# Two attention blocks: where the second sums of four weights are made, and which tiles hold them

## Chip, cores and metric

The kernel runs on one core of one Trainium2 chip. The metric is the device time of one execution, in microseconds (us). The kernel before was timed three times; one more execution was taken with the hardware profiler.

## The reference

The input x has 8 images of 512 channels and 32 x 32 = 1024 tokens. Two attention blocks follow each other:

```
layer 0: h = group_norm(x, 32 groups); q, k, v = w_qkv h + b      (8 heads of 64 channels)
         x = x + w_proj softmax(q k / 8) v + b_proj
layer 1: h = group_norm(x, 8 groups);  q, k, v = w h + b          (1 head of 512 channels)
         x = x + p_w softmax(q k / sqrt(512)) v + p_b
```

All of it is in 32-bit floating point.

## The kernel before

The matrix products with weights are not done directly. Each weight and each activation is split into 2 x 2 blocks, and seven products of sums of blocks replace eight products of blocks. `prepare(n)` loads a weight into a tile of the pool `wpool` and returns four steps, sums of its blocks on DVE (lines 285 and 286). For images after the first, the convolutions split once more: each of the seven operands is again cut into 2 x 2, with four further sums, the *second sums*. `keep2(n, t)` makes these for the weights v, q, k and m (four instructions of 128x896 on POOL, line 306) and stores the seven parts to DRAM, from which later images load them (line 308, seven DMAs called `sums_v`, `sums_q`, `sums_k`, `sums_m` in the profile; the profile calls the second sums by the name of the weight tile that they read, `prepare_v` and so on).

There are two pools that matter here. `big` has 32 tiles of 4 KB per partition and holds images, queries, keys, values, exponentials and factors. `wpool` has three tiles of 14 KB per partition and holds weights.

`prologue()` does the work before the first attention, in this order: load the layer 1 weights k and q and image 0, prepare v, q and k, multiply q and k to m (`product`, ps_wm), normalise image 0, make its block sums (`image_factors`, lines 170 to 173), then

- the value convolution of image 0 (`by_token`, bank names psa_v, psb_v, psc_v), whose steps p = 1, 2, 5, 6, 7, 4, 3 each run four pieces of a background list on DVE: the eight block sums of the image, then the first sums of q, then those of k,
- `keep2("v")`, the loads of image 1 for its statistics (x1, `bn_stats` at line 98),
- the q convolution (psa_q and so on), `keep2("q")` and `keep2("k")`,
- `prepare("m")` and the k convolution, with m's first sums between its steps, then `keep2("m")`,
- the load raw_p0, the transposes of layer 1's v weight (`natural`, tr_wv), their copies out of PSUM (natv, line 786, two on ACT and two on DVE), the mean of image 1 (gmean, d, d2, dv, lines 115 to 121), product z (ps_wz), products with biases.

In a convolution the sums u and w (line 238) go through DVE: the step p = 7 needs u, the step p = 4 needs w, since they share the PSUM bank b. After the prologue a loop over the images does attention of layer 0, projection, layer 1 of the image before, and the convolutions of the next one.

`tc.keep_in_program_order` pins an instruction behind what was traced before it on its engine. All other instructions are put into an order per engine when the program is built, and each engine then runs its own order, waiting where data or a tile isn't ready. A tile of a pool is used again when all users of its last contents are done.

Of the kernel before, what the change touches and what calls it, by code (L numbers as in the profile page):

```python
# [9 lines left out]
F32 = mybir.dt.float32  # L10
# [5 lines left out]
P = 128  # L16
# [13 lines left out]
def two_attention_blocks_kernel(  # L30
# [8 lines left out]
    nc = tc.nc  # L39
# [136 lines left out]
    def main_path(ctx):  # L176
        big = ctx.enter_context(tc.tile_pool(name="big", bufs=NBIG))
        wpool = ctx.enter_context(tc.tile_pool(name="wpool", bufs=3))
# [6 lines left out]
        def big_tile(name, shape=(P, T)):  # L185
            return big.tile(list(shape), F32, tag="big", name=name)
# [4 lines left out]
        def acc_tile(name):  # L191
            return ps_acc.tile([P, HT], F32, tag="acc", name=name)
# [14 lines left out]
        def load_x(b, c, what):  # L207
            t = big_tile(f"{what}_{b}_{c}")
            nc.sync.dma_start(t, x[b, c * P : (c + 1) * P, :])
            return t  # L210
# [12 lines left out]
        def finish():  # L223
            while tail:
                tail.pop(0)()
# [48 lines left out]
        def weight_factors(t):  # L274
            return {p: t[:, ORDER.index(p), :, :] for p in range(1, 8)}

        def prepare(n):
            t = wpool.tile([P, 7, 2, C // 2], F32, tag="w", name=f"prepare_{n}")
            half = lambda kh, mh: weights[n][ts(kh, C // 2), ts(mh, C // 2)].rearrange("(k p) m -> p k m", p=P)
            f = weight_factors(t)  # L280
            for p, kh, mh in ((1, 0, 0), (7, 0, 1), (4, 1, 1), (2, 1, 0)):
                nc.sync.dma_start(f[p], half(kh, mh))
            _, steps = left_sums(
                [(f[1], f[7])], [(f[2], f[4])], (lambda j: f[5], lambda j: f[6], lambda j: f[3]),
                lambda *a: tc.keep_in_program_order(nc.vector.tensor_add(*a)),
                lambda *a: tc.keep_in_program_order(nc.vector.tensor_sub(*a)),
            )
            return t, steps
# [4 lines left out]

        wdram2 = {n: dram.tile([P, 7, 7, P], F32, name=f"sums2_{n}") for n in "qkmv"}

        def keep2(n, t):

            u = [big_tile(f"prepare2_{n}_{i}", (P, 7, P)) for i in range(4)]
            quarter = lambda k, i: t[:, :, k, ts(i, P)]
            a11, a21, a12, a22 = quarter(0, 0), quarter(0, 1), quarter(1, 0), quarter(1, 1)  # L300
            s1, s2, s3, s4 = u
            for dst, x, y, op in (
                (s1, a21, a22, ALU.add), (s2, s1, a11, ALU.subtract), (s3, a11, a21, ALU.subtract),
                (s4, a12, s2, ALU.subtract),
            ):
                tc.keep_in_program_order(nc.gpsimd.tensor_tensor(dst, x, y, op))
            for j, f in enumerate((a11, a12, s4, a22, s1, s2, s3)):
                nc.sync.dma_start(wdram2[n][:, :, j, :], f)

# [31 lines left out]
        def image_factors(h, uid, sub=nc.vector.tensor_sub):  # L341

            tiles = [pair_tile(f"t{i}_{uid}") for i in (1, 2, 4)]
            halves = lambda t: (t[:, :HT], t[:, HT:])
            return right_sums(
                [halves(t) for t in h[:2]], [halves(t) for t in h[2:]],
                [lambda j, t=t: t[:, j, :] for t in tiles], sub,
            )
# [415 lines left out]
        def raw(n, i):  # L764
            ts_ = [pair_tile(f"raw{n}_{h}") for h in range(2)]
            for kc in range(KC):
                nc.sync.dma_start(ts_[kc // 2][:, kc % 2, :], w[i, ts(kc, P), :])
            return [ts_[kc // 2][:, kc % 2, :] for kc in range(KC)]
# [10 lines left out]
        def natural(wt, nm, banks):  # L779
            ts_ = [pair_tile(f"nat{nm}_{h}") for h in range(2)]  # L780
            t = [ts_[o // 2][:, o % 2, :] for o in range(KC)]
            pt = [ps_tile(banks[o // 2], f"tr_w{nm}_{o}") for o in range(KC)]
            for kc in range(KC):
                for o in range(KC):
                    transpose(pt[o][:, ts(kc, P)], wt[kc][:, ts(o, P)], ident)
            spread(lambda o, copy: tc.keep_in_program_order(copy(t[o], pt[o])), KC)
            return t

        def product(lhs, rhs, nm, hooks=()):

            hooks = dict(hooks)
            ts_ = [pair_tile(f"prod{nm}_{h}") for h in range(2)]
            for ic in range(KC):
                ps = ps_tile("a", f"ps_w{nm}_{ic}")
                for kc in range(KC):
                    matmul(ps, lhs[kc][:, ts(ic, P)], rhs[kc], start=(kc == 0), stop=(kc == KC - 1))
                    if ic * KC + kc in hooks:
                        hooks[ic * KC + kc]()
                nc.scalar.copy(ts_[ic // 2][:, ic % 2, :], ps)
                if ic % 2:  # L800
                    nc.sync.dma_start(
                        products[nm][ts(ic // 2, C // 2), :].rearrange("(kc p) o -> p kc o", p=P), ts_[ic // 2]
                    )
# [18 lines left out]
        def prologue():  # L822
            raw_k = raw("k", 5)
            raw_q = raw("q", 4)
            h0 = [load_x(0, c, "h0") for c in range(KC)]
            first = {n: prepare(n) for n in "vqk"}
            wk = natural(raw_k, "k", ("a", "b"))
            wq = natural(raw_q, "q", ("c", "acc"))
            norm = GroupNorm(0, "0_0", pinned=True)
            for c in range(KC):  # L830
                norm.stats(c, h0[c])
            hf, steps = image_factors(h0, "h0_0")

            def normed():
                norm.affine(acc_tile("gvar_0_0")[:, :KC])
                for c in range(KC):
                    norm.apply(nc.scalar if c % 2 else nc.gpsimd, h0[c], h0[c], c)

            product(
                wq, wk, "m", {6: lambda: norm.group_mean(acc_tile("gmean_0_0")[:, :KC]), 9: normed},  # L840
            )
            raw_v = raw("v", 6)
            raw_p = raw("p", 7)
            for f in first["v"][1]:
                f()
            background.extend(steps)
            for n in "qk":
                background.extend(first[n][1])
            v = by_token(weight_factors(first["v"][0]), hf, "v0_0", middle=(2, 5, 6, 7), back=4)
            finish()  # L850
            run_background(len(background))
            keep2("v", first["v"][0])
            x1 = [load_x(1, c, "x1") for c in range(KC)] if B > 1 else []
            norm1 = GroupNorm(0, "0_1")
            background.extend(lambda c=c: norm1.stats(c, x1[c]) for c in range(len(x1)))
            q = conv(weight_factors(first["q"][0]), hf, pcols("bq0"), "q0_0")
            keep2("q", first["q"][0])
            keep2("k", first["k"][0])
            t, steps = prepare("m")
            k = conv(weight_factors(first["k"][0]), hf, pcols("bk0"), "k0_0", hooks=[[], [], [], [], steps])  # L860
            finish()
            keep2("m", t)
            raw_p0 = raw("p0", 3)
            wv = natural(raw_v, "v", "bc")
            norm1.group_mean(acc_tile("gmean_0_1")[:, :KC])
            product(wv, raw_p, "z")
            norm1.affine(acc_tile("gvar_0_1")[:, :KC])
            bias = bias_products([(wk, "bq1"), (raw_p, "bv1"), (raw_p0, "bv0")])
            later = []
            for n in "pz":  # L870
                t, steps = prepare(n)
                later.append(steps)
                later.append([lambda n=n, t=t: keep(n, t), load_weight])
            later.append([
                lambda: tc.keep_in_program_order(nc.vector.tensor_copy(ubias, bias[0])),
                lambda: tc.keep_in_program_order(nc.vector.tensor_add(obias[1], bias[1], pcols("bp1"))),
                lambda: tc.keep_in_program_order(nc.vector.tensor_add(obias[0], bias[2], pcols("bp0"))),
                load_weight,
            ])
            return lambda s, head: v[s // 2][:, s % 2, ts(head, 64)], q, k, norm1, later  # L880

        psum_pools("first", 2)
        v, q, k, norm0, later = prologue()
# [141 lines left out]
        for b in range(B):  # L1025
# [18 lines left out]
            if b > 0:  # L1044
                hf, t = image_factors(h, f"h1_{b - 1}", here)
                for i, fs in enumerate((t[:1], t[1:2], (t[2], t[4]), (t[6], t[3]), (t[5], t[7]), steps[:2], steps[2:4])):
                    extra[2 * i + 3] += fs
            elif B > 1:
                hf, t = image_factors(h, "h0_1", here)
# [15 lines left out]
            if b > 0:  # L1065
                gf, gsteps = layer1_scores(b - 1, inner)
                _, _, mean, affine = norm_hooks(norm1, f"1_{b}")
# [7 lines left out]
                if b + 1 < B:  # L1075
                    v, norm0 = values(b + 1, made["inner"])
                    q, k = keys_and_queries(b + 1, made["inner"], norm0, ())
            elif B > 1:
                v, norm0 = values(1, inner)
# [217 lines left out]
```

## Time and profile before

| | us |
|---|---|
| median of 3 runs (lowest, highest) | 2845.38 (2845.05, 2845.61) |
| profiled execution, its own time | 2846.31 |
| its span | 2844.5 |
| PE busy | 2817.1 |
| DVE busy | 2129.8 |
| POOL busy | 1259.7 |
| ACT busy | 943.1 |
| first matmul of the value convolution of image 0 | 25.96 |
| first matmul of the q convolution | 59.03 |
| first matmul of product z | 114.33 |
| first matmul of the first attention's scores | 134.56 |

Times inside the span count from its start. The profiled execution's time is 1.8 us more than its span. PE is TensorE, DVE VectorE, ACT ScalarE, POOL GpSimd, SP SyncE, which issues nearly all DMAs here. A row in order of time gives start, duration, engine, line, operation and shapes; several equal instructions in a row are merged (x3). Rows by stretches give the length, then for PE, weight loads, DVE, ACT and POOL the busy us with the number of instructions, then the granted TensorE clock as a share, the busy share of the DMA engines, and GB/s.

### The profile page before, as it was taken

What the parts mean: (1) busy time and instruction counts of PE and PEld (TensorE: products, weight loads), DVE (VectorE), ACT (ScalarE), POOL (GpSimd) and SP (SyncE); (2) the same over time, 40 slices, a digit from 0 to 9 for tenths busy, and PEclk for the clock granted to TensorE, in tenths of its full rate; (3) what the DMA queues carried; (4) which work ended last, traced back from release to release, by engine and by line L of the source; (5) the groups of instructions that cost most, each with busy time, mean ns of one, the idle gap of its engine ahead of it and who ended that gap; (6) DMA issues with size and microseconds to landing.
All of it is one profiled execution on the core that took longest, in us unless ns stands there. A gap on an engine that the chain in (4) does not pass through costs nothing.

```text
span 2844.5 us, 33986 instructions
## 1 busy us (share of the span) xinstructions
PE 2817.1 (99%) x12434; PEld 1694.7 (60%) x12434; DVE 2129.8 (75%) x2873; ACT 943.1 (33%) x1205; POOL 1259.7 (44%) x1253
## 2 busy tenths in 40 slices
PE   8999999999999999999999999999999999999998
PEld 5434834867358663676536775376843768338584
DVE  6388688776887768777787777877678776887765
ACT  1153363313532145221452215522154212633130
POOL 4114224852258422574216741277313772147672
PEclk9999999999999999999999999999999999999999
DMA  8543402144030430313303232122411224112301
GB/s 285 166 153 110 185 20 95 47 156 163 18 123 21 173 148 20 138 49 149 128 24 130 100 117 110 48 105 112 146 72 49 101 108 155 42 45 101 119 4 68
DMA packets 98851, 291.68 MB, mean 103 GB/s; under 512 B 10803, under 2 KB 42867, under 8 KB 88950
## 3 DMA queue, kind: packets, MB, share of 16 engines
q1 hardware_dynamic: 96886, 287.16, 28.0%
q10 hardware_dynamic: 1792, 2.29, 0.2%
q8 instruction: 100, 1.64, 0.2%
q14 instruction: 73, 0.60, 0.1%
HBM read 236.94 MB, written 52.47 MB: 102 GB/s over the span
## 4 chain that ended last, share of the span: by engine, by line
PE 96%; DVE 2%; issue 1%; DMA 0%; ACT 0%; POOL 0%; SPq 0%; DVEq 0%; POOLq 0%; ACTq 0%
PE sc L67 16%; PE av L67 16%; PE psb_av L67 6%; PE psb L67 5%; PE psa_av L67 4%; PE psc_av L67 4%; PE psc L67 3%; PE psa L67 3%; PE psb_z L67 3%; PE psb_p L67 3%; PE psb_k L67 3%; PE psb_g L67 3%; PE psb_v L67 3%; PE psb_q L67 2%; PE psa_p L67 2%; PE psa_z L67 2%
## 5 line engine op out<-in xcount | busy, mean ns | idle before, releaser
L635 DVE TENSOR_TENSOR sum<-sum,e 128x1024 f32<-128x1024 f32 x384 | 518.7, 1351 | 41.4 <-DVE sum L635 1.4
L631 ACT ACTIVATE e<-sc 128x1024 f32<-128x1024 f32 x512 | 476.0, 1051 | 79.2 <-PE sc L67 79.2
L67 PE MATMUL sc<-q,k 64*128 64x512 f32 x2048 | 456.8, 596 | 0.0
L67 PE MATMUL av<-e,v 128*64 128x512 f32 x2048 | 453.6, 595 | 0.0
L67 PEld LDWEIGHTS sc<-q,k 64*128 64x128 f32 x2048 | 191.6, 186 | 238.5 <-ACT e L631 109.1
L67 PEld LDWEIGHTS av<-e,v 128*64 128x64 f32 x2048 | 141.4, 137 | 304.3 <-issue 304.3
L597 POOL TENSOR_TENSOR all_recs<-all_recs,rc 128x256 f32<-128x256 f32 x72 | 63.9, 888 | 543.5 <-DVE rc L595 543.5
L654 POOL TENSOR_TENSOR a<-a,r 128x512 f32<-128x512 f32 x56 | 113.7, 2031 | 260.8 <-DMA r<-rows 245.5
L595 DVE RECIPROCAL rc<-sums 128x256 f32<-128x256 f32 x72 | 126.5, 1757 | 46.1 <-PE sums L67 24.7
L649 ACT COPY a<-av 128x512 f32<-128x512 f32 x64 | 37.5, 586 | 321.7 <-PE av L67 321.7
L633 DVE TENSOR_TENSOR sum<-e,e 128x1024 f32<-128x1024 f32 x64 | 78.8, 1232 | 57.1 <-ACT e L631 57.0
L67 PE MATMUL psb<-inner,inner_h 128*128 128x256 f32 x448 | 116.1, 382 | 0.8
L67 PE MATMUL psa_av<-e,z 128*128 128x512 f32 x256 | 113.3, 595 | 0.0
L412 POOL TENSOR_TENSOR inner_h<-h,inner_h 128x256 f32<-128x256 f32 x120 | 109.1, 909 | 3.4
L140 ACT ACTIVATE h<-h,b,s 128x1024 f32<-128x1024 f32 x62 | 78.5, 1270 | 87.9 <-DMA h<-in_x 70.5
L67 PEld LDWEIGHTS psb<-inner,inner_h 128*128 128x128 f32 x448 | 83.9, 190 | 16.6 <-POOL inner L427 3.5
L412 POOL TENSOR_TENSOR inner_h<-h 128x256 f32<-128x256 f32 x60 | 56.7, 944 | 77.3 <-ACT h L140 77.3
L460 ACT COPY psb_v<-psa_v 128x512 f32<-128x512 f32 (+1 forms) x28 | 14.5, 517 | 223.9 <-DVE o L755 141.6
L695 POOL TENSOR_TENSOR sum<-sum,e 128x1024 f32<-128x1024 f32 x32 | 76.2, 2380 | 27.2 <-ACT e L691 26.0
L67 PE MATMUL psb_g<-inner_h,w_m 128*128 128x256 f32 x336 | 85.9, 383 | 0.3
L533 POOL TENSOR_TENSOR v<-v,v 128x256 f32<-128x256 f32 x28 | 20.1, 727 | 142.7 <-DVE u_v L528 142.7
L412 POOL TENSOR_TENSOR inner_h<-t_h 128x256 f32<-128x256 f32 x90 | 79.1, 885 | 9.0 <-DVE t_h L170 9.0
(364 smaller groups left out, 5736.6 us busy)
## 6 DMA issues: line engine op xcount, KB each, us to landing
x<-in_x SPq DMA_DIRECT2D x36, 512.0 KB
h<-in_x SPq DMA_DIRECT2D x32, 512.0 KB
spill<-x SPq DMA_DIRECT2D x32, 512.0 KB
h<-spill SPq DMA_DIRECT2D x32, 512.0 KB
x<-spill SPq DMA_DIRECT2D x32, 512.0 KB
out<-x SPq DMA_DIRECT2D x64, 256.0 KB
w_p<-sums_p SPq DMA_DIRECT2D x8, 1792.0 KB
r<-rows SPq DMA_DIRECT2D x112, 128.0 KB
```

Source lines behind the costliest of these rows:

```text
L67: tc.keep_in_program_order(nc.tensor.matmul(*args, **kw))
L140: tc.keep_in_program_order(nc.scalar.activation(dst, src, AF.Identity, bias=b, scale=s))
L412: pin(nc.gpsimd.tensor_tensor(dst, x, y, ALU.subtract))
L533: nc.gpsimd.tensor_tensor(d, x, y, ALU.add)
L595: nc.vector.reciprocal(rc, sums)
L597: nc.gpsimd.tensor_tensor(all_recs, all_recs, rc, ALU.add)
L631: nc.scalar.activation(e, sc, AF.Exp, scale=(C // 8) ** -0.5)
L633: nc.vector.tensor_add(total, es[0], e)
L635: nc.vector.tensor_add(total, total, e)
L649: nc.scalar.copy(dst, av)
L654: nc.gpsimd.tensor_tensor(dst, dst, r, ALU.mult)
L695: on = lambda dst, x, y: lambda: tc.keep_in_program_order(nc.gpsimd.tensor_tensor(dst, x, y, ALU.add))
```

## The change

`keep2` gets an engine as an argument. With the default, POOL, its four sums go into one tile of `wpool` instead of four of `big`; so it is for q, k and m. For v it is called with VectorE: there the sums stay in four `big` tiles and are made by DVE, pinned at the place of the call, which is behind the last outputs of image 0's value convolution.

```diff
-        def keep2(n, t):
-
-            u = [big_tile(f"prepare2_{n}_{i}", (P, 7, P)) for i in range(4)]
+        def keep2(n, t, engine=nc.gpsimd):
+
+            if engine is nc.gpsimd:
+                u = wpool.tile([P, 4, 7, P], F32, tag="w", name=f"prepare2_{n}")
+                u = [u[:, i, :, :] for i in range(4)]
+            else:
+                u = [big_tile(f"prepare2_{n}_{i}", (P, 7, P)) for i in range(4)]
...
-                tc.keep_in_program_order(nc.gpsimd.tensor_tensor(dst, x, y, op))
+                tc.keep_in_program_order(engine.tensor_tensor(dst, x, y, op))
...
-            keep2("v", first["v"][0])
+            keep2("v", first["v"][0], nc.vector)
```

## The prediction

> **What bounds the kernel now.** I read the shares of the page first, then the chain of waits in order of time, then DVE, POOL and SP in order of time round the two places where the chain leaves PE early on, and last the busy time by stretches of 10 us. The page's chain, by engine:
>
> ```profile
> PE 96%; DVE 2%; issue 1%; DMA 0%; ACT 0%; POOL 0%; SPq 0%; DVEq 0%; POOLq 0%; ACTq 0%
> ```
>
> So only a PE gap that goes away shortens the span, and a new cost counts only where it opens one. From the first scores (134.6 us) to 269 us the chain is PE alone; the diff acts before that. There the chain has two holes (start, us, what):
>
> ```profile
> 45.44 3.15 DVE prepare_k L286 x2
> 48.60 0.61 DVE w_v L238
> ...
> 49.25 6.48 PE psb_v L67 x16
> ...
> 110.64 3.68 issue
> 114.33 16.65 PE ps_wz L67 x32
> ```
>
> Hole A: the value convolution waits for DVE, which still makes the k weights' first sums ahead of w_v. Hole B: product z waits for the copies of the transposed v weights (natv). DVE and POOL at these places (start, us, line, operation, shapes):
>
> ```profile
> 43.07 5.53 DVE L286 TENSOR_TENSOR prepare_k<-prepare_k 128x512 f32<-128x512 f32 x3
> ...
> 110.09 1.30 DVE L117 TENSOR_TENSOR d<-mv,gmean 128x4 f32<-128x4 f32 x1
> 111.43 2.00 DVE L119 TENSOR_TENSOR d<-d 128x4 f32<-128x4 f32 x1
> ...
> 113.54 1.28 DVE L786 COPY natv<-tr_wv 128x512 f32<-128x512 f32 x2
> ```
>
> ```profile
> 44.94 2.51 POOL L306 TENSOR_TENSOR prepare_q<-prepare_q 128x896 f32<-128x896 f32 x1
> ...
> 111.34 2.07 POOL L306 TENSOR_TENSOR prepare_m<-prepare_m,prepare_m 128x896 f32<-128x896 f32 x1
> ```
>
> The same 128x512 sum takes 0.68 us at 37.6 us, where POOL is idle, and 1.7 to 2.6 us at 26.4 to 36.4 and 41.3 to 48.6 us, where POOL makes the second sums of v and q (25.93 to 35.9 and 40.41 to 47.5 us). A 128x4 operation of 0.16 us takes 1.30 and 2.00 us at 110 us and ends when a POOL sum ends. POOL runs second sums of v from 25.93 us, far before their place in the program, since nothing stands ahead of them there. Each hole then costs more than its idle time:
>
> ```profile
> 50.00:60.00 10.00, 10.00 (x35) 8.00 (x34) 3.76 (x6) 0.00 (x0) 4.58 (x3) 0.76 0.94 267
> ...
> 110.00:120.00 10.00, 5.67 (x7) 2.46 (x8) 4.72 (x6) 0.63 (x2) 3.41 (x2) 0.66 0.60 183
> ```
>
> The granted clock (third from the end) falls to 0.76 and 0.66. Sixteen psb_v matmuls take 6.48 us instead of the 3.45 us of the next sixteen, and the 32 of product z 16.65 us instead of 32 x 0.429 = 13.73 (eight such take 3.43 us).
>
> **What the skill says.** SBUF — State Buffer, "Who interferes with whom": a DVE instruction with two SBUF inputs and a GpSimd one that reads SBUF exclude each other, and the later one blocks until the other ends; one with at most one SBUF input does not. The trace agrees on both: the rows above, and v<-psb_v,t_v (one input in PSUM) keeps 0.69 us at 55.77 beside a POOL sum at 55.34. TensorE: Matmul & The Clock Gate, "What's actually happening": after an idle window of about 3.4 us the clock halves until PE has been busy as long. The gaps of 4.69 and 4.47 us with their slow matmuls agree; the gap of 0.83 us at 40.0 shows none. VectorE: DVE Perf Modes, the errata section, gives (N+151)/0.96 ns for an fp32 tensor_tensor; the trace has 0.69 us at 512 and 1.225 us at 1024, as the formula does.
>
> **The change, part by part.**
>
> (1) POOL loses the four v sums (9.97 us at 25.93 to 35.9). The q sums now need a weight tile. The pool has three, held by v, q and k weights; the first to come free is v's, after the value convolution and the stores of its sums. So POOL stands idle from 25.9 to about 56 us, and the eight image sums, four q sums and four k sums on DVE run at 0.68 us. From 26.42: L171, L172, L173 end at 30.5, q at 33.2. PE's order is kept: psb_v p=6 runs 36.4 to 39.9; u_v is ready at 38.9 and 40.6; k sums 40.6 to 43.3; w_v at 44.0. PE p=7 ends at 43.3, waits 0.7 us, p=4 ends at 47.5 and p=3 at 50.9, without a slow clock. Before, q's first matmul started at 59.03. Gain 8.1 us: gaps of 0.83 and 4.69 shrink to 0.7, the clock gives 2.9 to 3.0, the rest is rounding of ends.
>
> (2) DVE gains four 128x896 sums behind v's last outputs: estimate (896+151)/0.96 = 1.09 us each, 4.4 us, 51.6 to 56.0. Bounds: 1.07 (1.225 us scaled by 896/1024) to 2.5 (what a DVE sum took at most beside POOL's, which has no work then); the work itself can't bring a gain. Behind them wait the statistics of x1 and u_q. PE needs u_q only for psb_q p=7, 13.7 us after q starts, at 64.6: slack 8, cost 0. Without that cover it would be 4.4.
>
> (3) The seven v stores keep their number; three need no sums. The other four are issued on SP from about 53 to 58 us (5.48 us for four before), and x1's four loads (3.94 us) behind them to 62, 2 us later than before while PE is 8 earlier. If the x1 statistics stay ahead of u_q in DVE's order, the first x1 (6.7 us from issue to use before) and its 1.5 us of statistics put u_q at about 66: a stall of 0 to 2 us. I take 0, since u_q's input is ready first.
>
> (4) q's sums on POOL: 56 to 64.3 (4 x 2.08), stores to about 70; k's take that tile again, 70.5 to 78.8, stores issued by about 81. The m loads take the tile of q (q convolution ends at 86.5 - 8.1 = 78.5) or that of k's sums (82). Four issues (4.26 us) and landing: 85 to 90 us. DVE wants them at 101.88 - 8.1 = 93.8: slack 4 to 9, cost 0. DVE beside POOL's q and k sums does one-SBUF-input work, so it isn't slowed. The m sums then find a free tile by 82; p's loads take k's tile at 99 and are used at 130.
>
> (5) Twelve of the large tiles fewer are asked for after v. SP in order of time:
>
> ```profile
> 86.69 1.92 SPq L282 DMA_DIRECT2D prepare_p<-in_w  x4
> 105.05 12.22 SPq L308 DMA_DIRECT2D sums_m<-prepare_m  x7
> 117.32 3.75 SPq L767 DMA_DIRECT2D rawp<-in_w  x4
> ```
>
> The last row is raw_p0, read straight from an input, yet it stands behind sums_m although SP was idle for 16 us before these. And natv's DVE copies, traced ahead of the mean's operations, stand behind them in DVE's order. I read both as tiles being given in program order: raw_p0's and natv's come after the four large tiles of the m sums. With m, q and k sums out of that pool they follow k's tiles directly, so natv's copies can stand ahead of the mean's four operations. They read PSUM and so don't mind POOL. Product z then starts about 0.7 us after the transposes (product m: 0.46 after) instead of 4.5: 3.8 to 4.0 us, plus 2.9 of clock: 6.8. Bounds of this part: 0 (order stays) and 7.2. POOL's m sums stay beside d and d2, which are needed only when product z ends.
>
> Sum: 8.1 + 6.8 = 14.9 us off the profiled execution's 2846.31 (span 2844.5 and 1.8 around it), which is 0.9 above the median: median 2845.4 - 14.9 = 2830.5. Later loads keep their place relative to PE, so the gain is kept.
>
> **Rivals.** *Order stays*: part (5) gives nothing, hole B remains with its clock; only 8.1: 2837.3. For it: the order is fixed at build by expected times that the page doesn't show. Against: the SP row. *Gain partly returned to DVE or SP*: u_q or w_q waits for late x1 statistics, 2 to 4 us: 2832.5 to 2834.5. For it: x1 moves later while PE moves earlier; against: 8 us of slack. *Weight tiles become the bound, slower*: if m's loads get the k weights' tile, they start when the k convolution ends, at 99.0, land at about 105.3, and DVE makes m's sums till 108, k's last outputs till 110.2; the transposes, held by k's banks, start 2 us later than now, POOL's m sums fall on 108 to 116.3, and with natv still behind the mean's operations product z starts at about 117 instead of 114.3, with cold transposes up to 1.6 more: +3 to +4, 2849. It decides from about 109 us as the time at which DVE gets m's sums done; below, there is still a gain. Against it: q's tile and that of k's second sums are free 17 us earlier. *Not done*: the pieces could be reordered so that POOL still contends in hole A; its tile is not free before v ends, so I give that almost nothing.
>
> **Numbers.** A measurement of this kernel can tell about 0.2% (5.7 us) from no change. Forecast with both holes closed, 0.58; order stays, 0.20; partly returned, 0.09; weight tiles bind, 0.08; anything within 5.7 us, 0.05. Faster 0.85, same 0.07, slower 0.08 (a little of the tile rival ends near zero, and something unseen may cost). The range takes in parts (5) at 7.2 and a further 3 us of reordering below, and the rival at 2837.3 with 3.7 us above: 2826 to 2841.
>
> **What would show it.** L171, L172 and prepare_k at about 0.68 us; q's first matmul at about 51; no POOL sum between 26 and 55 us and four DVE ones of 128x896 at about 1.09 us behind v; natv's copies ahead of d, product z at about 102 us lasting 13.8; granted clock near 1 in both stretches; first scores at about 119.7 instead of 134.56. It is wrong if prepare_m's sums on DVE wait for their loads, if u_q waits behind x1's statistics, or if natv still stands behind d.

## The result, and the profile after

| | before | after |
|---|---|---|
| median of 5 runs each, us (lowest, highest) | 2845.6 (2845.05, 2846.86) | 2831.35 (2831.03, 2832.98) |
| profiled execution, its own time, us | 2846.31 | 2831.03 |
| its span, us | 2844.5 | 2829.2 |
| PE busy, us | 2817.1 | 2811.2 |
| first scores of the first attention, us | 134.56 | 119.44 |
| from there to the end of the span, us | 2709.9 | 2709.8 |

The ratio is 0.9951, interval 0.9936 to 0.9965: 14.2 us less at the medians, 15.3 us in the profiled executions, of which 15.1 lie ahead of the first scores. Behind them the time is the same to 0.2 us.

The page's chain by engine, after:

```profile
PE 97%; DVE 1%; issue 1%; POOL 0%; ACT 0%; DVEq 0%; POOLq 0%
```

The chain in order of time, after (start, us, what), at the places of the two holes:

```profile
42.99 0.61 DVE w_v L238
43.60 0.04 issue
43.65 3.72 PE psb_v L67 x16
...
101.19 0.59 ACT natv L790
101.79 0.09 issue
101.88 13.97 PE ps_wz L67 x32
```

Where 16 matmuls took 6.48 us they now take 3.72, and the 32 of product z take 13.97 instead of 16.65. The 3.68 us of "issue" ahead of product z are 0.09. DVE in order of time, after (start, us, line, operation, shapes; in brackets idle time before it and its releaser):

```profile
41.10 1.89 DVE L286 TENSOR_TENSOR prepare_k<-prepare_k 128x512 f32<-128x512 f32 x3
...
51.47 1.08 DVE L310 TENSOR_TENSOR prepare_v<-prepare_v 128x896 f32<-128x896 f32 x1
...
54.60 1.08 DVE L310 TENSOR_TENSOR prepare_v<-prepare_v,prepare_v 128x896 f32<-128x896 f32 x1
...
57.80 0.69 DVE L238 TENSOR_TENSOR u_q<-psb_q,t_q 128x512 f32<-128x512 f32 x1 [1.03 <-PE psb_q L67]
63.61 1.29 DVE L98 BATCH_NORM_STATS2 bnst<-x 128x6 f32<-128x512 f32 x2 [5.12 <-DMA x<-in_x]
...
68.99 0.67 DVE L238 TENSOR_TENSOR w_q<-psb_q,t_q 128x512 f32<-128x512 f32 x1
...
101.08 1.29 DVE L790 COPY natv<-tr_wv 128x512 f32<-128x512 f32 x2 [1.41 <-PE tr_wv L70]
...
103.07 2.00 DVE L119 TENSOR_TENSOR d<-d 128x4 f32<-128x4 f32 x1
```

Read it from the top. Three first sums of k take 1.89 us, where before three took 5.53. The second sums of v begin on DVE at 51.47 at 1.08 us each. The block sum u_q comes ahead of the statistics of x1, w_q behind them. The copies natv come first, and d, slow again beside POOL's m sums, comes after them, where nobody waits for it. All of POOL's second sums, after:

```profile
55.82 8.30 POOL L310 TENSOR_TENSOR prepare_q<-prepare_q 128x896 f32<-128x896 f32 x4 [30.20 <-DMA sums_v<-prepare_v]
72.65 8.32 POOL L310 TENSOR_TENSOR prepare_k<-prepare_k 128x896 f32<-128x896 f32 x4 [8.53 <-DMA sums_q<-prepare_q]
96.73 8.32 POOL L310 TENSOR_TENSOR prepare_m<-prepare_m 128x896 f32<-128x896 f32 x4 [15.76 <-DVE prepare_m L286]
```

POOL has no work from 25.6 to 55.8 us: the q sums wait for v's weight tile. The bracket names a store of v's sums, but the three stores that read that tile were issued by 32 us. What ends late is DVE's last sum of v, which reads the tile too: it ends at 55.68, and the q sums begin 0.14 us behind it. With four and twelve more sums on DVE (third question) it is the same 0.14 us (55.96 to 56.10, 55.94 to 56.08).

The saving, from the first matmul of each stage on PE:

| stretch | before | after | saved |
|---|---|---|---|
| start to the value convolution | 25.96 | 25.61 | 0.35 |
| value convolution to q convolution | 33.07 | 25.05 | 8.02 |
| q convolution to product z | 55.30 | 51.22 | 4.08 |
| product z, busy | 16.65 | 13.97 | 2.68 |

These make 15.13, and 134.56 - 119.44 = 15.12. The first row is scatter: nothing in the diff acts there, and over the ten profiles of this document the value convolution starts at 25.61 to 26.42 us.

### The profile page after: what moved, and what is told of

Same layout as the page of the kernel before. It is cut to its first block, busy times and chain, and to the rows that moved or that the text cites. A ratio compares the mean times of both kernels' runs of the same rounds, so it can differ in the third digit from the quotient of the medians.

```text
span 2829.2 us, 33980 instructions
## 1 busy us (share of the span) xinstructions
PE 2811.2 (99%) x12434; PEld 1691.7 (60%) x12434; DVE 2119.0 (75%) x2877; ACT 942.7 (33%) x1205; POOL 1250.6 (44%) x1249
## 4 chain that ended last, share of the span: by engine, by line
PE 97%; DVE 1%; issue 1%; POOL 0%; ACT 0%; DVEq 0%; POOLq 0%
PE sc L67 16%; PE av L67 16%; PE psb_av L67 6%; PE psb L67 5%; PE psa_av L67 4%; PE psc_av L67 4%; PE psc L67 3%; PE psa L67 3%; PE psb_z L67 3%; PE psb_p L67 3%; PE psb_k L67 3%; PE psb_g L67 3%; PE psb_v L67 3%; PE psb_q L67 2%; PE psa_p L67 2%; PE psa_z L67 2%
## 5 line engine op out<-in xcount | busy, mean ns | idle before, releaser
L637 DVE TENSOR_TENSOR sum<-e,e 128x1024 f32<-128x1024 f32 x64 | 78.8, 1231 | 57.0 <-ACT e L635 57.0
L67 PE MATMUL psb_g<-inner_h,w_m 128*128 128x256 f32 x336 | 85.9, 383 | 0.3
L685 DVE TENSOR_TENSOR e<-psc,u 128x512 f32<-128x512 f32 x56 | 38.7, 691 | 59.0 <-PE psc L67 58.6
```

The costliest lines, as they stand in the source:

```text
L67: tc.keep_in_program_order(nc.tensor.matmul(*args, **kw))
L637: nc.vector.tensor_add(total, es[0], e)
L685: nc.vector.tensor_add(dst[0], ps, x[0])
```

## Experiments

**First question: which half of the change closes which hole?** The theory was that POOL's second sums beside DVE's cost hole A, and that the program order in which `big` hands out tiles costs hole B. Rivals: the sums' engine as such matters, or the holes have other causes. The runs of this group share a before of 2845.74 us (median of 29 runs).

*The tiles alone.* v's sums stay on POOL in four `big` tiles; q, k and m take weight tiles. Against the kernel after:

```diff
-            if engine is nc.gpsimd:
+            if n != "v":
...
-            keep2("v", first["v"][0], nc.vector)
+            keep2("v", first["v"][0])
```

> The tile half alone: the second sums of q, k and m in weight tiles, those of v still on POOL in large tiles. Theory (a DVE sum with two SBUF inputs is held by whatever POOL sum runs beside it, and each hole closes when POOL's sums leave that stretch): v's sums still slow L171 and L172 to about 2.6 us each, but they end at about 35.6, q's sums wait for v's tile, so the k sums on DVE run at 0.68 us and w_v is ready at about 45; the q convolution starts at about 51.6 (50.66 with the whole change), hole B is closed: about 2832.3 us. Rival (it is the v sums' move to DVE that closes hole A, the tiles only hole B): q starts at 59, 2838.7.

Measured 2833.15 us (2832.28 to 2834.28), ratio 0.9958 (0.9942 to 0.9975). The theory's 2832.3 held, the rival's 2838.7 did not. DVE in order of time in this kernel:

```profile
31.86 5.05 DVE L172 TENSOR_TENSOR h<-h,h 128x512 f32<-128x512 f32 x2
...
42.48 1.89 DVE L286 TENSOR_TENSOR prepare_k<-prepare_k 128x512 f32<-128x512 f32 x3
```

The image's block sums are still slow (2.5 us each) beside POOL's v sums, but that has slack. The k sums are at full speed, because POOL's q sums must wait for v's weight tile (they start at 52.34). So hole A came from the **q sums** on POOL, not the v sums: value convolution to q convolution is 25.62 us, against 25.05 after. PE still waits 0.83 us for u_v, as before, but not for w_v. Hole B is closed too: product z takes 13.97 us. In this stretch the move of v's sums to DVE saves 0.6 us more, less than the times can tell.

*The engine alone.* All second sums stay in `big` tiles; v's are made by DVE.

```diff
-            if engine is nc.gpsimd:
+            if False:
```

> The engine half alone: v's second sums on DVE behind v's convolution, those of q, k and m on POOL in large tiles. Theory: POOL makes three q sums at about 32.4 to 38.7 us, when DVE waits for PE, the fourth waits for a tile of v's sums; so the k sums on DVE are free and hole A closes (q starts at about 50.7). The large tiles of m's sums still stand ahead of raw_p0 and natv, so natv's DVE copies stay behind d and hole B stays with its slow clock: 2845.5 - 8.1 = 2837.4. Rival (natv comes ahead since the whole prologue is earlier): 2831. Rival (q's sums on POOL run into the k sums): q starts at 54 to 56, about 2842.

Measured 2838.26 us (2837.47 to 2839.03), ratio 0.9973 (0.9964 to 0.9983): the theory's 2837.4. POOL in order of time shows why hole A closes in this one too, and PE why hole B does not:

```profile
56.11 2.08 POOL L310 TENSOR_TENSOR prepare_q<-prepare_q,prepare_q 128x896 f32<-128x896 f32 x1 [17.22 <-DMA sums_v<-prepare_v]
```

```profile
106.04 16.23 PE L67 MATMUL ps_wz<-rawp,natv 128*128 128x512 f32 x32 [4.46 <-issue]
```

Without the four v sums ahead of them, three of the q sums run from 32.61 to 38.9 us and are out of the way of the k sums; the fourth waits for a tile that v's stores hold. So either half closes hole A, in its own way, and the two don't add up there.

*Only the order of the tiles.* The kernel before, with m's second sums written down behind natv's tiles and the mean of image 1. Against the kernel before:

```diff
-            keep2("m", t)
             raw_p0 = raw("p0", 3)
             wv = natural(raw_v, "v", "bc")
             norm1.group_mean(acc_tile("gmean_0_1")[:, :KC])
+            keep2("m", t)
```

> The kernel before with one statement moved: the second sums of m are traced behind the transposes of v and the mean, all second sums on POOL in large tiles as before. Theory (tiles are given in program order, so m's four large tiles hold back raw_p0 and natv when the order is made): natv's copies stand ahead of d, product z starts 0.4 to 0.7 us behind the transposes and lasts 13.8 us, hole A is as before: 2845.5 - 6.8 = 2838.7. Rival (order set by something else): 2845.5.

Measured 2839.82 us (2838.17 to 2842.17), ratio 0.9979 (0.9972 to 0.9987): 5.9 us less, 6.3 at the first scores, where the theory had 6.8. SP, DVE and PE in order of time:

```profile
89.03 1.89 SPq L767 DMA_DIRECT2D rawp<-in_w  x4
...
105.43 9.62 SPq L308 DMA_DIRECT2D sums_m<-prepare_m  x7
```

```profile
109.89 1.29 DVE L786 COPY natv<-tr_wv 128x512 f32<-128x512 f32 x2 [1.46 <-PE tr_wv L70]
```

```profile
110.68 13.97 PE L67 MATMUL ps_wz<-rawp,natv 128*128 128x512 f32 x32 [0.44 <-ACT natv L786]
```

The load raw_p0 is issued at 89.03 instead of 117.32, natv's copies have nothing to wait for, and product z starts 0.44 us after the transposes. Hole A is there as before (4.69 us of waiting, 6.73 for the matmuls behind it). The engine alone and the order alone are worth 7.5 and 5.9 us, 13.4 together; from this group's before to the change's 2831.35 it is 14.4. These are two holes with two causes, and each part of the prediction's sum stands alone.

Hole B lay in the order that was built, not in a wait for a tile while the kernel ran: before, ACT's two copies natv, which write into the same two tiles as DVE's, ran at 109.56 us, while DVE's stood behind d until 113.54.

**Second question: does it matter that DVE makes v's sums?** The tiles alone nearly do it, with v's sums early on POOL. Here, against the kernel after, they are put back on POOL in `big` tiles, but held until the value convolution is done, by a 128x4 POOL operation that reads v's last outputs, so the sums come where the change puts them, only on the slower engine.

```diff
-            if engine is nc.gpsimd:
+            if n != "v":
...
-            keep2("v", first["v"][0], nc.vector)
+            held = small.tile([P, 4], F32, tag="held", bufs=1, name="held")
+            tc.keep_in_program_order(nc.gpsimd.tensor_tensor(held, v[3][:, 1, 0:4], v[2][:, 1, 0:4], ALU.add))
+            keep2("v", first["v"][0])
```

> The whole change, but v's second sums on POOL, held behind the last outputs of v's convolution by one small POOL operation that reads them (4 elements, its result unused). Theory (what matters is that no POOL sum runs beside DVE's first sums, not which engine makes v's): q starts at about 50.7; v's sums on POOL 52 to 60, q's to 70, k's to 84, m's loads still in time for 93.5: 2831 to 2832, as with the change. Rival (DVE's double speed is needed, since v's tile comes free 4 us later and x1 later too): w_q or m's sums are late, 2834 to 2840.

Measured 2835.55 us (2834.41 to 2838.79), ratio 0.9967 (0.9954 to 0.9979). My theory missed, the rival was right. SP, DVE and PE in order of time:

```profile
54.48 7.45 SPq L312 DMA_DIRECT2D sums_v<-prepare_v  x4
61.99 3.40 SPq L209 DMA_DIRECT2D x<-in_x  x4
```

```profile
68.17 1.28 DVE L98 BATCH_NORM_STATS2 bnst<-x 128x6 f32<-128x512 f32 x2 [9.10 <-DMA x<-in_x]
```

```profile
75.13 3.70 PE L67 MATMUL psb_q<-t_h,prepare_q 128*128 128x512 f32 x8 [3.10 <-DVE w_q L238]
```

v's four stores are issued as the sums come, x1's loads stand behind them on SP, and x1's statistics stand ahead of w_q on DVE. PE waits 3.10 us for w_q. In the kernel after, PE in order of time:

```profile
71.26 3.60 PE L67 MATMUL psb_q<-t_h,prepare_q 128*128 128x512 f32 x8
```

There x1's statistics start at 63.61, w_q is done at 69.66 and PE wants it at 71.26: **1.6 us of slack**. That is the tightest cover of the change that was found.

*The same with x1's loads first.* x1's loads are written down ahead of v's held sums (`held` as in the run before).

```diff
-            if engine is nc.gpsimd:
+            if n != "v":
...
-            keep2("v", first["v"][0], nc.vector)
             x1 = [load_x(1, c, "x1") for c in range(KC)] if B > 1 else []
+            held = ...
+            keep2("v", first["v"][0])
```

> As the kernel with v's second sums on POOL behind v's convolution (2835.6, with a PE wait of 3.10 us for w_q), but the four loads of x1 are traced ahead of v's second sums. Theory (that wait came from x1's loads, which stood on SP behind the stores of v's sums, so that x1's statistics ended late ahead of w_q in DVE's order): the wait is gone, 2832.4. Rival (POOL's slower sums themselves delay something in the q convolution): 2835.6.

Measured 2837.34 us (2834.26 to 2838.67), ratio 0.9965 (0.9952 to 0.9978); this and the later runs share a before of 2845.87 us. w_q is done at 67.5 and PE does not wait for it, as the theory said. But the time did not fall to the theory's 2832.4: the next thing was late. SP, DVE and PE in order of time:

```profile
91.66 1.92 SPq L282 DMA_DIRECT2D prepare_m<-product_m  x4
```

```profile
98.45 0.69 DVE L285 TENSOR_TENSOR prepare_m<-prepare_m 128x512 f32<-128x512 f32 x1 [4.45 <-DMA rawp<-in_w]
```

```profile
102.33 0.33 PE L70 MATMUL tr_wv<-ident,rawv 128*128 128x128 f32 x1 [2.13 <-DVE k L392]
...
105.81 15.16 PE L67 MATMUL ps_wz<-rawp,natv 128*128 128x512 f32 x32
```

The weight tiles are a chain: q's sums start when v's last sum is done (61.19 us here, 55.82 after), and k's sums when q's stores have landed (77.75 here, 72.65 after). Here m's loads take the tile of k's sums: SP waits 3.6 us for k's stores to land and issues the loads at 91.66. In the kernel after, they don't wait for that landing; they follow k's last store on SP at once. SP and DVE in order of time, after:

```profile
74.76 7.46 SPq L312 DMA_DIRECT2D sums_k<-prepare_k  x4
82.74 3.18 SPq L282 DMA_DIRECT2D prepare_m<-product_m  x4
85.97 1.89 SPq L771 DMA_DIRECT2D rawp<-in_w  x4
```

```profile
93.46 0.68 DVE L285 TENSOR_TENSOR prepare_m<-prepare_m 128x512 f32<-128x512 f32 x1
```

With x1's loads first, m's first sums come late and hold up k's last outputs on DVE, and the transposes wait 2.13 us for a bank. Product z then takes 15.16 us, 1.2 more than with the change, and the first scores come at 124.56. That is like the prediction's slower rival, but milder: the tile was that of k's sums, not that of the k weights. With the change the loads have landed at about 90.9 us (behind the row of rawp, which ends at 87.86, SP waits 3.0 us more for them) and are used at 93.46: **about 2.6 us of slack**.

**Third question: how much DVE work behind v does the change bear?** Extra 128x896 sums into a tile that nothing reads, behind v's own:

```diff
+            return u
...
-            keep2("v", first["v"][0], nc.vector)
+            u = keep2("v", first["v"][0], nc.vector)
+            more = big_tile("more", (P, 7, P))
+            for _ in range(4):
+                tc.keep_in_program_order(nc.vector.tensor_tensor(more, u[0], u[1], ALU.add))
```

*Four more.*

> The whole change with four more 128x896 sums on DVE behind v's second sums, into a tile that nothing reads (the doubled cost). If v's four sums cost nothing since DVE idles there (5.1 us ahead of x1's statistics), these cost nothing either: 2831.4. If each microsecond of DVE there were on the path: 2835.7.

Measured 2833.52 us (2832.14 to 2834.0), ratio 0.9955 (0.9939 to 0.997). In the prologue they cost almost nothing: the step p = 4 of the q convolution starts at 71.65, 0.1 us late counted from its step p = 7. DVE in order of time shows that they were not the 1.08 us each that I had put them at:

```profile
60.37 5.25 DVE L860 TENSOR_TENSOR more<-prepare_v,prepare_v 128x896 f32<-128x896 f32 x2
```

Two of them ran beside POOL's q sums at 2.6 us each, and a third took 2.37. Most of the rest of the difference lies behind the first scores, in the clock (last section).

*Twelve more.*

> The same with twelve more sums, five ahead of x1's statistics and seven among them. Theory: what is late first is w_q behind the statistics, whose slack in the profile is about 1.6 us, and not u_q with its 8: seven sums of 1.05 us put w_q at about 77 where PE wants it at 71.3, a wait of 5 to 6 us and up to 2.9 us of slow clock behind it: 2836.5 to 2840.5. If the prediction's slack of 8 us at u_q were the one that binds, 12.6 - 8.5 gives a wait of 4 us on u_q and none on w_q.

Measured 2846.94 us (2845.95 to 2848.43), ratio 1.0005 (0.9996 to 1.0013): the whole gain is gone. PE in order of time:

```profile
83.61 5.48 PE L67 MATMUL psb_q<-t_h,prepare_q 128*128 128x512 f32 x8 [11.92 <-DVE w_q L238]
```

DVE in order of time:

```profile
60.35 8.12 DVE L860 TENSOR_TENSOR more<-prepare_v,prepare_v 128x896 f32<-128x896 f32 x3
...
77.13 2.35 DVE L860 TENSOR_TENSOR more<-prepare_v,prepare_v 128x896 f32<-128x896 f32 x1
```

The place was as expected: w_q, not u_q, which had no wait. The size was not: 11.92 us of waiting where 5 to 6 were expected, and 1.9 us of slow clock behind it (5.48 instead of 3.60). I had taken every sum at 1.05 us, but six of the twelve ran beside POOL's q and k sums, at 2.3 to 2.9 us.

**Fourth question: can the last 0.53 us of hole A go?** Four empty entries in the background list put k's first sums behind w_v.

```diff
-            for n in "qk":
-                background.extend(first[n][1])
+            background.extend(first["q"][1])
+            background.extend([lambda: None] * 4)
+            background.extend(first["k"][1])
```

> The whole change with the first sums of the k weights one step later in the background list, behind w_v instead of ahead of it. The last wait in hole A (0.53 us of PE for w_v) goes: q starts at about 50.1, 0.5 us less, 2830.8. If the k sums then hold back v's last outputs, nothing or 0.5 us more.

PE in order of time has no wait left in the value convolution:

```profile
43.25 3.62 PE L67 MATMUL psb_v<-prepare_v,t_h 128*128 128x256 f32 x16
```

The stretch to the q convolution is 24.25 us instead of 25.05, the first scores come at 118.93 instead of 119.44. The time is 2832.22 us (2830.63 to 2832.98), ratio 0.9951 (0.9938 to 0.9965), the same as that of the change: half a microsecond is below what these times can show.

## Why the prediction was right

2830.5 us was predicted and 2831.35 measured, with the sum of 14.9 against 15.1 ahead of the first scores, of which 0.35 is scatter at the start. Step by step:

- **Part (1), hole A**: 8.1 predicted, 8.02 measured. The wait left is 0.53 us, where 0.7 was predicted. The slow matmuls of the two holes lost 2.76 and 2.68 us (2.9 to 3.0 and 2.9 predicted), of the 5.9 by which PE's busy time fell in all. The last of the k sums before, at 47.92 us, took 0.68 and not 1.7 to 2.6; POOL's sum beside the others had ended at 47.45. The tiles alone showed one thing finer than the prediction had it: the q sums on POOL made the hole, and the v sums had only pushed them there. What the Trainium skill says under SBUF — State Buffer, "Who interferes with whom", agrees here too: the k sums, with two SBUF inputs, take 0.63 us each once POOL is idle, and u_q, with one, keeps its 0.69 us at 57.80 beside POOL's q sums.
- **Part (2), DVE's sums**: predicted at 1.09 us from 51.6 to 56.0; measured 1.08 from 51.47 to about 55.7, hidden. The cover was named wrongly. The text put u_q's slack of 8 us there, and that holds: PE wants u_q at about 64.4, the sums end at 55.7 and u_q takes 0.69, which leaves 8.0. But behind DVE's sums, v's stores and x1's loads stands also **w_q, with 1.6 us**. The prediction did not work out when w_q was wanted; only a rival named it, at 0.09. That this cover held was luck, as far as the prediction goes.
- **Part (3), SP's order**: x1's loads are issued from 56.64 to 60.3 us, and u_q stayed ahead of x1's statistics, as taken. The stall was 0. The rival "partly returned" is what the run with v's sums held on POOL did: 3.1 us of waiting, at w_q.
- **Part (4), the weight tiles**: q's sums 55.8 to 64.1 (56 to 64.3 predicted), k's 72.65 to 81.0 (70.5 to 78.8 predicted), m's loads issued 82.74 to 85.9. The prediction had v's tile come free with v's stores; it was v's last sum, at the same time, since v's sums were put at 56.0. The step of 2 us on k's sums is the stores of q's sums, issued until 69.0 and released at 72.6, which the prediction had as "to about 70". m's loads landed at about 90.9 and were used at 93.46 (85 to 90 and 93.8 predicted): the slack is about 2.6 us, below the 4 to 9 given. The term that was too small is the way from issue to landing: the loads follow k's stores on SP, which ended at 82.22 and not by about 81, and they land 8.2 us behind their first issue. The run with x1's loads first used the slack up, so loads of m that wait for a weight tile do cost time; the change does not reach that.
- **Part (5), hole B**: 6.8 predicted; 4.08 of starting earlier and 2.68 of clock measured, 6.76. The guess at its cause, the program order of tiles, was tested apart: writing m's sums down later, in the kernel before, closes the same hole.

The rival "order stays" (2837.3) is the kernel with the engine alone, 2838.26. The low end of the range is 1 us lower than its terms give: 2845.4 - 8.1 - 7.2 - 3 is 2827.1, not 2826.

## What to carry over

At a DVE stall beside POOL work, check which piece of POOL's work stands beside it. Here it was the q sums, and there were two ways out: to hold them back (a tile that is not yet free did it), or to take the v sums away ahead of them, so that they ran earlier. Where tiles of a pool are handed out in program order, an operation that is written down late can be put late in its engine's order by tiles that another engine uses late, though its own data is there; a load that is issued behind stores while its queue was idle shows it. When work is hidden, work out the slack of everything behind it in that engine's order, not of the first waiter alone: here it was 1.6 us at w_q, against 8 at u_q. And a bracket that names a store need not be the releaser: see what else that reads the tile ended last.

## What the runs showed of the hardware

Two things were not expected. First, the price of DVE and POOL sums side by side: a 128x896 DVE sum takes 2.3 to 2.9 us instead of 1.08, and a POOL sum as much as 2.9 instead of 2.08 (11.45 for four). Both sides lose.

Second, the clock. The time behind the first scores is 2709.7 to 2710.5 us in seven of the ten profiles, but 2711.7 with v's sums held on POOL, 2711.3 with x1's loads first and 2712.3 with four more sums. Most of the difference lies where the value convolution of image 1 waits twice on PE, within 3 us of each other: 0.64 to 0.66 and 1.16 us, alike in all ten. From the matmuls between these two gaps to the next group of psc_v it is 9.41 us in these three and 7.78 or 7.79 in the seven. The same stretch of the kernel with four more sums and of the kernel after (length, then PE, weight loads, DVE, ACT and POOL busy, then the granted clock, the DMA share, GB/s):

```profile
260.50:280.50 20.00, 18.09 (x127) 16.34 (x126) 18.02 (x40) 3.17 (x6) 3.85 (x5) 0.91 0.60 206
```

```profile
260.00:280.00 20.00, 18.09 (x142) 16.34 (x141) 18.63 (x42) 3.46 (x7) 5.40 (x7) 1.00 0.67 232
```

The clock was 0.91 in one and 1.00 in the other, with the same idle time. PE in order of time, the group behind the second gap, in the same two kernels:

```profile
267.10 2.08 PE L67 MATMUL psb_v<-w_v,inner_h 128*128 128x128 f32 x8 [1.16 <-ACT u_v L455]
```

```profile
266.61 1.16 PE L67 MATMUL psb_v<-w_v,inner_h 128*128 128x128 f32 x8 [1.16 <-ACT u_v L454]
```

Eight matmuls take 2.08 us instead of 1.16 behind equal gaps (1.78 and 1.83 in the other two). The Trainium skill, TensorE: Matmul & The Clock Gate, "What's actually happening", has the clock fall after an idle window of about 3.4 us. The gaps of 4.69 and 4.47 us before fit that, and so does the gap of 3.10 us without a slow group behind it (3.70 us, with v's sums held on POOL). Gaps of 0.64 and 1.16 us with a fall in three profiles and none in seven do not. Nor does the run with x1's loads first: ahead of its slow product z (15.16 us) PE waited 0.51, 2.13, 0.33 and 0.33 us with one transpose of 0.33 us between each two, so no gap was near 3.4 us. So short gaps close together can slow the clock, and sometimes do not. What decides it stays open. The same section has the windows run freely, so it may depend on where the gaps fall in them; no run here shows that. For this work it means that 1.6 us between two of these kernels can come from there, with nothing in their prologues to explain it.
